# Cross-attention with layer norm: score products of 32 rows instead of 64

## The chip, the core and the metric

The kernel runs on one NeuronCore of a Trainium2 chip. The metric is the time of one execution on the device in microseconds. Five engines work side by side, each through its own list of instructions in order: PE (TensorE, with its weight loads shown apart as PEld), DVE (VectorE), ACT (ScalarE), POOL (GpSimd) and SP (SyncE, which here only issues transfers).

## The reference, cut to what matters

```python
qs  = (q @ wq).reshape(B, S, 16, 32).transpose(0, 2, 1, 3)      # q: 4 x 2048 x 512
ks_ = (k @ wk).reshape(B, 77, 16, 32).transpose(0, 2, 1, 3)     # k = v: 4 x 77 x 512
vs  = (v @ wv).reshape(B, 77, 16, 32).transpose(0, 2, 1, 3)
scores = einsum('bhqd,bhkd->bhqk', qs, ks_) / sqrt(32)
scores = where(mask[:, None, :, :], -inf, scores)
attn_w = softmax(scores, axis=-1)
attn = einsum('bhqk,bhkd->bhqd', attn_w, vs)
out  = attn.transpose(0, 2, 1, 3).reshape(B, S, 512) @ wo + q
return layernorm(out) * gamma + beta
```

There are 8,192 query rows, 16 heads of 32 channels, and 77 keys for each of the four batches. The scores are, for each head and query row, a sum over only 32 channels.

## The kernel before

The 8,192 rows are worked on as 64 tiles of 128 rows. Keys and values are made once at the start. Queries are projected for four tiles at a time (`q_rows`, L276), transposed: a head's 32 channels lie on 32 partitions, four heads above each other, so that `q_g` holds heads in four groups of rows (`j` = 0 to 3) and four groups along its free dimension (`g` = 0 to 3). The weights and activations of the large products are split into a high and a low part and multiplied in three terms.

For one tile these steps follow each other, on several engines:

- `scores` (L406, PE): 16 heads by 77 keys. The queries are the loaded operand, the keys `kct` the moving one, 77 columns. The products read 32 partitions, so they take 32 of the array's rows; the rows of the tile are taken `SR` at a time, and each product writes `SR` partitions of one of four banks of PSUM (`sc[j]`, one bank for each group of partitions). With `SR` = 64 there are 32 products for a tile, in eight places of the array (4 groups of rows x 2 groups of 64 columns).
- `maxima` (L423, DVE): adds the mask, negates and copies the scores of one head to SBUF and gives their minimum; 16 instructions for a tile. The banks come free with it.
- `exps` (L438, ACT): 16 exponentials with row sums.
- `recip` and `normalise` (L448 DVE, L453 POOL), then `transp` (L474, DVE) transposes in blocks of 32, and twelve transfers for two tiles (`regroup_part`, L485) put the keys on partitions.
- `av` (L499, PE): weights by values for two tiles, 96 rows by 32 columns of the array for each product, four places side by side; then ACT and DVE split the result (L528, L532).
- `o_proj` (L555, PE): 12 products of 128 x 512 for a tile, then residual, layer norm and store on DVE, POOL, ACT and SP.

The order of all this on all engines is written out by hand in one list of words (`ORDER`): `S5` are the scores of tile 5, `T5.0` to `T5.3` its maxima, `V2` the value products of tiles 4 and 5, `O7` the output projection of tile 7, `Q14` a part of a query projection. A second table (`SLOTS`) names the buffer or the PSUM bank that each tile gets. In most places PE's list has one `S` between other products; four times two stand in a row (S0 S1, S2 S3, S6 S7, S56 S57). An instruction that needs a bank waits in PE's list until DVE or ACT has read it.

The products of one tile are issued by this loop; `SR` is the constant that the change touches, and nothing else in the program uses it:

```python
        for g in range(NG):
            for r0 in range(0, P, SR):
                for j in range(GH):
                    q = slice(HD * j, HD * (j + 1))
                    mm = nc.tensor.matmul(
                        sc[j][r0 : r0 + SR, g * NK : (g + 1) * NK],
                        qs[q, g, rs.start + r0 : rs.start + r0 + SR],
                        kct[q, g, t // TPB, keys_of(j)],
                        start=True,
                        stop=True,
                    )
```

The innermost loop goes over the four groups of partitions `j`, the next over the rows of the tile, the outermost over the four groups of heads.

Of the kernel before, what the change touches and what calls it, by code (L numbers as in the profile page):

```python
# [38 lines left out]
MASKED = -3.38e38  # L39
EPS = 1.0e-5  # L40
WARM = 9
SR = 64
NPB = 3
KSCALE = 1.0 / HD**0.5
LAST = 56
# [129 lines left out]
def xattn_layernorm(  # L175
# [75 lines left out]
    def keys_of(h):  # L251
        return slice(TAIL_K, NK2) if h % 2 == 0 else slice(0, NK)
# [145 lines left out]
    def scores(t):  # L398
# [3 lines left out]
# [8 lines that stand above are left out]
# [388 lines left out]
```

## Time and profile before

| | before |
|---|---|
| median of 2 runs | 511.21 us (510.82 to 511.6) |
| profiled execution | 511.52 us |
| its span, first to last instruction | 509.7 us |
| mean granted TensorE clock | 0.996 |
| PE busy | 499.7 us, 6,833 matmuls, as many loads |
| DVE, ACT, POOL busy | 468.1, 465.1, 420.9 us |
| HBM traffic | 41.79 MB read, 16.78 MB written |

How to read the profile: a line of a group names the source line, the engine, the operation, and written tile <- read tiles; for PE the form `32*64` is how many rows and columns of the array the product takes, `32x77` what moves through it. Behind it stand the count, the busy time and the mean of one, and the idle time of the engine ahead of these instructions with what ended it. A row of waits names who waited for what, the total in us, how often, and the longest. PE's matmuls overlap: the next one starts while the one before is still running out, so the sum of their durations is more than the time they take. A tile's score products stand in the trace as a burst, a row of loads and matmuls of line 406 without anything between.

### The profile page before, as it was taken

How to read it: one execution, taken by the hardware profiler on the slowest of the kernel's cores; microseconds unless marked ns; L12 is line 12 of the kernel's file. 1: busy time of each engine (PE TensorE's matmuls, PEld its weight loads, DVE VectorE, ACT ScalarE, POOL GpSimd, SP SyncE). 2: the span in 40 equal slices, each digit the busy share in tenths (PEclk: the TensorE clock that was granted, in tenths of full speed). 3: DMA queues.
4: the chain of work that ended last, by engine and by line, in shares of the span. 5: the costliest groups of instructions: out<-in, count | busy, mean ns of one | idle time of the engine just before them, and what ended most of it. 6: DMA issues, size and time to landing. Idle time of an engine off the chain costs nothing. (4 is left out here: it accounts for less than half of the span.)

```text
span 509.7 us, 20305 instructions
## 1 busy us (share of the span) xinstructions
PE 499.7 (98%) x6833; PEld 383.9 (75%) x6833; DVE 468.1 (92%) x2559; ACT 465.1 (91%) x2222; POOL 420.9 (83%) x387
## 2 busy tenths in 40 slices
PE   8999999999999999999999999999999999999994
PEld 6987878777777778777777777777777777777773
DVE  6799989998998989889989998999999999999997
ACT  6699999999999999998999999999999999989620
POOL 3656566866897999997998898998999899998895
PEclk9999999999999999999999999999999999999998
DMA  8947877778688975879787878787978688689655
GB/s 297 395 169 204 184 202 185 187 184 241 185 232 232 253 214 144 231 214 270 215 251 200 219 187 236 192 223 194 249 215 209 194 225 236 194 220 255 160 187 215
DMA packets 58781, 110.85 MB, mean 217 GB/s; under 512 B 9462, under 2 KB 11278, under 8 KB 58678
## 3 DMA queue, kind: packets, MB, share of 16 engines
q1 hardware_dynamic: 55222, 102.75, 72.4%
q0 software_dynamic: 2496, 5.77, 4.2%
q10 hardware_dynamic: 960, 1.05, 0.8%
q8 instruction: 54, 0.88, 0.8%
q14 instruction: 49, 0.40, 0.3%
HBM read 41.79 MB, written 16.78 MB: 115 GB/s over the span
## 5 line engine op out<-in xcount | busy, mean ns | idle before, releaser
L438 ACT ACTIVATE pbuf<-pbuf,nm 128x77 f32<-128x77 f32 x1024 | 352.7, 352 | 8.0 <-DVE nm L423 7.7
L438 ACT ACTIVATION_READ_ACCUMULATOR pbuf<-pbuf,nm 128x1 f32 x1024 | 197.3, 193 | 0.0
L423 DVE CUSTOM_DVE_ANT_0 pbuf<-sc,mb 128x77 f32<-128x77 f32 x1024 | 170.2, 233 | 6.9 <-PE sc L406 4.8
L453 POOL TENSOR_TENSOR pbuf<-pbuf,ri 128x1232 f32<-128x1232 f32 x63 | 142.4, 2264 | 34.1 <-DVE ri L448 28.6
L474 DVE STREAM_TRANSPOSE B<-pbuf 128x1280 f32<-128x1280 f32 x64 | 95.9, 1500 | 9.2 <-POOL pbuf L453 7.0
L555 PE MATMUL po<-woh,AH 128*128 128x512 f32 x256 | 104.0, 406 | 0.1
L276 PE MATMUL pq<-xth,wqh 128*128 128x512 f32 (+1 forms) x256 | 100.6, 393 | 0.8 <-DVE nm L423 0.7
L555 PE MATMUL po<-wol,AH 128*128 128x512 f32 x256 | 100.0, 391 | 0.0
L555 PE MATMUL po<-woh,AL 128*128 128x512 f32 x256 | 99.9, 390 | 0.0
L276 PE MATMUL pq<-xtl,wqh 128*128 128x512 f32 (+1 forms) x256 | 98.2, 383 | 0.0
L276 PE MATMUL pq<-xth,wql 128*128 128x512 f32 (+1 forms) x256 | 98.1, 383 | 0.0
L423 DVE DVE_READ_ACCUMULATOR2_ANT nm<- 128x1 f32 x1024 | 85.9, 84 | 0.0
L270 POOL TENSOR_TENSOR xtl<-xtf,xth 128x1024 fp32r<-128x1024 f32 x28 | 67.4, 2406 | 10.5 <-ACT xth L266 7.2
L596 POOL TENSOR_TENSOR o<-o,gam 128x512 f32<-128x512 f32 x56 | 72.2, 1294 | 2.6 <-ACT o L593 2.6
L599 POOL TENSOR_TENSOR o<-o,bet 128x512 f32<-128x512 f32 x56 | 72.0, 1291 | 1.4
L406 PEld LDWEIGHTS sc<-kct,q 32*64 32x64 f32 x4096 | 51.7, 130 | 22.2 <-issue 12.0
L406 PE MATMUL sc<-kct,q 32*64 32x77 f32 x4096 | 61.3, 238 | 0.3 <-DVE nm L423 0.2
L499 PE MATMUL pa<-PT,vsb 96*32 96x256 f32 x992 | 59.7, 382 | 0.2 <-DMA PT<-B 0.2
L555 PEld LDWEIGHTS po<-woh,AH 128*128 128x128 f32 x256 | 48.0, 188 | 15.2 <-issue 3.2
L276 PEld LDWEIGHTS pq<-xth,wqh 128*128 128x128 f32 x256 | 48.1, 188 | 14.7 <-issue 2.5
L555 PEld LDWEIGHTS po<-woh,AL 128*128 128x128 f32 x256 | 48.1, 188 | 10.6
L276 PEld LDWEIGHTS pq<-xth,wql 128*128 128x128 f32 x256 | 48.1, 188 | 9.8
(99 smaller groups left out, 638.2 us busy)
## 6 DMA issues: line engine op xcount, KB each, us to landing
PT<-B SPq DMA_DIRECT2D x343, 128.0 KB
xtf<-xT SPq DMA_DIRECT2D x28, 512.0 KB
o<-x SPq DMA_DIRECT2D x56, 256.0 KB
out<-o SPq DMA_DIRECT2D x56, 256.0 KB
PT<-B POOLq DMA_DIRECT2D x25, 128.0 KB, 4.8
stage_a<-kin SPq DMA_DIRECT2D x4, 410.0 KB
xtf<-xT SPq DMA_DIRECT2D x4, 256.0 KB
wq_f<-wq SPq DMA_DIRECT2D x4, 256.0 KB
```

The lines of the kernel that those rows point to most:

```text
L270: return nc.gpsimd.tensor_tensor(l[:, c : c + 2], fx.pop((g, c)), xh[g][:, c : c + 2].bitcast(F32), ALU.subtract)
L276: nc.tensor.matmul(pq, w[:, c, m * P : (m + 1) * P], r[g][:, c, rs], start=(n == 0), stop=(n == 11))
L406: mm = nc.tensor.matmul(sc[j][r0 : r0 + SR, g * NK : (g + 1) * NK], qs[q, g, rs.start + r0 : rs.start + r0 + SR], kct[q, g, t // TPB, keys ...
L423: nc.vector.tensor_tensor_reduce(pb[:, h // 2, (h % 2) * NK : (h % 2 + 1) * NK], scs[t][j][:, g * NK : (g + 1) * NK], mb[:, t % TPB, keys_ ...
L438: nc.scalar.activation(pb[:, h // 2, (h % 2) * NK : (h % 2 + 1) * NK], pb[:, h // 2, (h % 2) * NK : (h % 2 + 1) * NK], AF.Exp, bias=nmax[t ...
L453: return nc.gpsimd.tensor_tensor(pv, pv, rv.to_broadcast((P, NP, 2, NK)), ALU.mult)
L474: nc.vector.transpose(bt.rearrange("p c q r -> p q c r"), pbuf[t % NPB].rearrange("p q (c r) -> p q c r", c=5),)
L499: nc.tensor.matmul(pas[b, g // 2][HD * j : HD * (j + 1), (g % 2) * BLK : (g % 2 + 1) * BLK], vsb[:, 2 * b // TPB, h % 2, HD * (h // 2) : H ...
L555: nc.tensor.matmul(pos[t], a[:, c, rs], w[:, c, :], start=(first and c == 0 and n == 0), stop=(c == NC_D - 1 and n == 2),)
L596: return nc.gpsimd.tensor_tensor(od[t], od[t], gam, ALU.mult)
L599: return nc.gpsimd.tensor_tensor(od[t], od[t], bet, ALU.add)
```

## The change

One constant: the rows of a tile that one score product takes.

```diff
 EPS = 1.0e-5
 WARM = 9
-SR = 64
+SR = 32
 NPB = 3
```

The loop over `r0` now takes four steps instead of two. Each product loads 32 columns of queries instead of 64 and writes 32 partitions instead of 64; the keys that move through are the same 77 columns. A tile has 64 products instead of 32, and they lie in sixteen places of the array (4 groups of rows x 4 groups of 32 columns) instead of eight. All products of one group `j` still write one bank, and the sixteen products of one `g` follow each other before the next `g`. The words of the order, the banks and buffers, and the lists of the other engines are what they were; on PE's list 5,850 program matmuls stand where 3,802 stood, and each of the new ones stands beside the one that it was cut from or four places on.

## The prediction

> **What bounds the kernel now.** I read the busy table first, then the same busy times by stage, then who waits for whom, and last the inside of one burst of score products.
>
> ```profile
> PE 499.7 (98%) x6833; PEld 383.9 (75%) x6833; DVE 468.1 (92%) x2559; ACT 465.1 (91%) x2222; POOL 420.9 (83%) x387
> ...
> 0.00:20.00 20.00, 18.57 (x123) 15.83 (x124) 12.84 (x27) 12.84 (x26) 7.11 (x19) 1.00 0.95 336
> 20.00:465.00 445.00, 443.81 (x6381) 340.17 (x6381) 415.69 (x2435) 432.89 (x2124) 377.46 (x316) 1.00 0.79 214
> 465.00:509.70 44.70, 37.37 (x343) 27.95 (x340) 39.58 (x100) 19.34 (x75) 36.32 (x53) 0.96 0.67 195
> ```
>
> The columns of the windows are the stretch, its length, then PE, weight loads, DVE, ACT and POOL (busy time and number of instructions), the granted clock, and the DMA. From 20 to 465 us, where all scores lie (20.9 to 465.6, in line 406's row below), TensorE is busy 443.8 of 445.0 us. ACT has 432.9 us of work there and DVE 415.7, so they are close behind, but behind.
>
> A busy PE could still be a waiting PE, so the waits come next:
>
> ```profile
> PEld sc L406 <- issue: 12.0, 34, 0.4
> PEld sc L406 <- DVE nm L423: 6.0, 15, 0.5
> DVE pbuf L423 <- PE sc L406: 4.8, 11, 1.0
> ```
>
> The idle time of weight loads ahead of scores is about 0.35 to 0.4 us each time, whoever is named: this is the pause in which the array empties before the first 32-row load, and it comes once per burst. No single wait is longer than 0.5 us. TensorE works through its order and waits for nobody; whatever makes its part of one tile longer is added to the end, 64 times.
>
> Now the line that changes, its loads, and the one other place with 32-column loads:
>
> ```profile
> L406 PEld LDWEIGHTS sc<-kct,q 32*64 32x64 f32 x4096 | 51.7, 130 | 22.2 <-issue 12.0 <-DVE nm L423 6.0 <-DVE ri L448 0.8
> L406 PE MATMUL sc<-kct,q x4096: 222/225/277, 20.9 to 465.6; 32*64 32x77 f32 x196
> L499 PEld LDWEIGHTS pa<-PT,vsb x992: 106/110/110, 68.4 to 485.2; 96*32 96x32 f32 x199
> L499 PE MATMUL pa<-PT,vsb x992: 376/379/403, 68.4 to 485.4; 96*32 96x256 f32 x199
> ```
>
> The program has 64 tiles x 32 = 2,048 score products, the trace 4,096 pairs of a load and a matmul: each f32 product runs as two pairs, a first pass and a second pass in the same place of the array. One burst is 64 pairs:
>
> ```profile
> 205.06 0.80 PEld L406 LDWEIGHTS sc<-kct,q 32*64 32x64 f32 x64 [0.35 <-PE pq L276]
> 205.06 0.95 PE L406 MATMUL sc<-kct,q 32*64 32x77 f32 x64
> ```
>
> That is 0.95 us from first start to last end; a matmul takes 0.225, so the last starts 0.726 us after the first. How these starts lie is read from windows that all begin at 205.00, before the burst, so that the counts (matmuls, then loads) add up:
>
> ```profile
> 205.00:205.11 0.11, 0.05 (x8) 0.05 (x8) 1.00 0.86 261
> 205.00:205.16 0.16, 0.10 (x8) 0.10 (x16) 1.00 0.58 176
> 205.00:205.19 0.19, 0.13 (x10) 0.13 (x18) 1.00 0.55 172
> 205.00:205.38 0.38, 0.32 (x33) 0.32 (x33) 1.00 0.83 226
> 205.00:205.43 0.43, 0.37 (x33) 0.37 (x34) 1.00 0.78 219
> 205.00:205.44 0.44, 0.38 (x33) 0.38 (x35) 1.00 0.76 214
> 205.00:205.48 0.48, 0.42 (x37) 0.42 (x37) 1.00 0.75 213
> 205.00:205.68 0.68, 0.62 (x54) 0.62 (x61) 1.00 0.80 223
> 205.00:205.80 0.80, 0.74 (x64) 0.74 (x64) 1.00 0.80 225
> ```
>
> Three rates are in here. **Start rate**: 16 loads from 205.06 to 205.16, 15 gaps of 6.7 ns. **Place rate**: from 205.19 to 205.38 23 matmuls start in 0.19 us, 8.3 ns each, that is one round of all eight places per 0.067 us. Then the third: by 205.38 33 loads have begun, the 34th just after, and then nothing until the 35th at 205.44. From 205.48 to 205.68 the loads come at 24 in 0.20 us, 8.3 ns each, so one product (two loads) per 16.7 ns; this is a **supply rate**, since the first of these go to places that stand idle and still come one product at a time.
>
> Why does the 35th load wait? Four times two tiles' bursts stand behind one another; one such pair shows whether the pause repeats:
>
> ```profile
> 420.50:420.52 0.02, 0.00 (x0) 0.00 (x0) 1.00 0.62 205
> 420.50:420.55 0.05, 0.01 (x3) 0.02 (x3) 1.00 0.52 164
> 420.50:420.90 0.40, 0.36 (x33) 0.37 (x34) 1.00 0.12 31
> 420.50:420.92 0.42, 0.39 (x35) 0.39 (x35) 1.00 0.11 29
> 420.50:421.28 0.78, 0.74 (x67) 0.75 (x68) 1.00 0.06 16
> 420.50:421.30 0.80, 0.77 (x69) 0.77 (x69) 1.00 0.06 15
> ...
> 421.77 0.52 PE L406 MATMUL sc<-kct,q 32*64 32x77 f32 x25
> ...
> 420.50:422.10 1.60, 1.56 (x128) 1.57 (x128) 1.00 0.29 111
> ```
>
> Load 1 starts at 420.54, load 35 at 420.91 (between 420.90 and 420.92), load 69 at 421.29. So load n+34 comes 0.375 us after load n, twice in a row, and the same 0.375 separates 205.06 from 205.44. I read it as a **window**: 34 pairs, or 17 products, are all that may be under way, and a product leaves it when its second pass has ended. The parts fit: second pass begins 0.117 us after the product's first load (the ninth matmul, between 205.16 and 205.19), lasts 0.225, and some 0.03 is left for the next to arrive: 0.375.
>
> **The change, part by part.** Each of the 32 products of a tile becomes two of 32 rows: 64 products, 128 pairs, per tile; 8,192 pairs in all in place of 4,096. The moving operand stays at 77 columns, the loads shrink from 64 to 32 columns, the places go from eight to sixteen. No other engine gets or loses an instruction, no transfer and no bank changes, and the order is the same.
>
> What shrinks: the first load before the first pass. It shows as 277 against 225 ns at L406, 52 ns with 64 columns, and as 403 against 379 at L499, 24 ns with 32. So a second pass starts 0.117 - 0.027 = 0.090 us after its product's first load, and the window's turn is 0.375 - 0.027 = 0.348 us. Later loads run under matmuls and cost nothing; without that cover it would be 0.02 to 0.05 us for each pass, and the place rate above shows the cover is there (0.067 us a round, with a 0.131 us load per matmul).
>
> What the sixteen places give: the place rate no longer binds, since 17 products hardly more than fill the array once. What then binds is the window. Counting products from 0: product 17 begins at 0.348 us, product 34 at 0.696, product 51 at 1.044, each after the window's turn; inside each batch the products come 16.7 ns apart (17 x 16.7 = 0.284, shorter than the turn, so the turn decides). Product 63 is the twelfth after 51: 1.044 + 12 x 0.0167 = 1.244. Its second pass: + 0.090 = 1.334 us.
>
> The same bookkeeping on the burst of before, to test it: product 17 at 0.375, product 31 fourteen later, + 0.234, + 0.117 for its second pass: 0.726. Measured: 0.726.
>
> So a burst grows from 0.726 to 1.334 us, by 0.608. The pause ahead (0.35) and the emptying behind it stay. All 64 count, since TensorE is the bound in the whole stretch: 64 x 0.608 = 38.9 us. In the four pairs that stand back to back the batches run on (128 products: product 119 at 7 x 0.348 = 2.436, eight more at 16.7 ns, + 0.090 = 2.66, against 1.53 now, 421.77 + 0.52 - 0.225 - 420.54), which is 1.13 in place of 1.22 more: -0.3 us for all four. Sum: 38.6 us.
>
> The work of DVE on a tile (L423) waits for the tile's scores and will begin 0.6 us later each time; that shows as idle time of DVE, and costs nothing while PE is the bound: DVE's 415.7 and ACT's 432.9 us stand in a stretch that grows to some 484. Nothing stands behind it but the softmax of that tile, whose results PE needs several bursts later.
>
> Bounds. From below: if only the start rate held, 127 x 6.7 ns = 0.851, + 0.125, 64 times + 8.0 us. From above: the nearest row to 128 pairs is the back-to-back pair of tiles, 1.53 us on eight places with a wait for banks in it: + 0.80, 64 times + 51 us. I take the window's value between them, since it repeats twice and gives 0.726 for the burst of before.
>
> The profiled execution took 511.52 us (span 509.7, the rest around it), 0.3 above the median of 511.21; I work from its own time: 511.5 + 38.6 = **550 us**.
>
> A rule speaks against this. The Trainium skill, TensorE: Matmul & The Clock Gate, Part 3: Packing small matmuls, gives a pack's span as one matmul plus about 4 ns for each further tile, and its measured gain is largest with all sixteen tiles. By it 128 pairs would need an estimated 0.225 + 127 x 0.004 = 0.73 us, less than the 0.95 that 64 pairs take now. The trace does not bear it out here: no gap below 6.7 ns in the burst, and 8.3 after it.
>
> **The rivals.**
>
> *The array decides after all; faster.* Mechanism: 128 pairs on sixteen places are eight rounds, as 64 on eight are. Without the window a burst is 0.090 + six more rounds of 0.067 + sixteen starts of a last round at 4.2 ns (0.067/16) = 0.56 us, 0.17 less than now: 64 x 0.17 = 10.9, **500.6 us**. It decides from a mean start gap below 0.726/127 = 5.7 ns. For it: the place rate of 0.067 does bind in the first half of a burst now. Against it: 6.7 ns is the shortest gap, even at L499's 32-column loads, and the 35th load waits with places idle. Faster than some 499 it cannot be, since ACT's 432.9 us leave 12 of the 445. That rule of the skill would land here.
>
> *Only the start rate; no change.* If small products leave the window as fast as they start: + 8.0 us, **519.5**. Against it: the supply rate.
>
> *The supply rate alone.* One pause, then 16.7 ns a product without a second one: 0.348 + 46 x 0.0167 + 0.090 = 1.206 us, + 0.48, 64 times 30.7: **542**. For it: a single burst of before shows only one pause. Against it: load 69 at 421.29; but a wait for a bank stands near it and could be what I see.
>
> *The worse side.* Loads that do not get shorter leave the turn at 0.375: product 51 at 1.125, 63 at 1.325, end 1.442: + 0.716, 45.8 us, **557**. And fetching code:
>
> ```profile
> q8 instruction: 54, 0.88, 0.8%
> ```
>
> 0.88 MB for 13,666 loads and matmuls is 64 B each, so 8,192 more are 0.52 MB, 32 more fetches of 16 KB. A fetch lasts 0.008 x 16 x 509.7/54 = 1.2 us; if every new one were waited for, + 39 us on top, **589**. Against it: 54 are hidden now.
>
> **How the numbers follow.** Window: 0.62, 550 (its own range 546 to 554). Supply alone: 0.18, 542. Start rate alone: 0.06, 519.5. Array decides: 0.03, 500.6. The worse side: 0.11, mostly 557. The range 536 to 559 takes in the window, the supply case with a shorter first pause, and the longer loads, and leaves out the two cheap cases, the fetches and the upper bound. A measurement of this kernel can tell about 2% (10 us) from no change: faster 0.03, same 0.06, slower 0.91, from the same cases.
>
> **What would show it.** Right: line 406 with 8,192 pairs of form 32*32, loads of 106 to 110 ns in place of 130, bursts of about 1.56 us in place of 0.95; in cumulative counts, pauses before loads 35, 69 and 103, 0.35 us apart; PE still busy over 97% from 20 to some 500 us; DVE waiting for scores longer than 4.8 us in all. Supply alone: one pause, bursts of 1.43. Start rate alone: 1.08 and no pause. Wrong altogether: bursts below 0.95 us, or bursts as I say and a PE that had idle time to give, which the waits of weight loads would then show gone.

## The result, and the profile after

| | before | after |
|---|---|---|
| median of 2 runs | 511.21 us | 601.64 us (598.02 to 605.27) |
| ratio | | 1.1767 [1.173, 1.1805] |
| profiled execution, its span | 511.52, 509.7 us | 598.02, 596.2 us |
| mean granted clock | 0.996 | 0.980 |
| PE busy | 499.7 us (98%) | 555.5 us (93%) |

Runs that lie more than 1.5% above the fastest of the same kernel count as slow, and times are compared without them.

The change makes the kernel 18% slower, 90 us. The prediction said slower, but by 38.6 us and to at most 559: it missed by 52 us. The page of the profile after, its busy table, its line of code fetches, and the groups of the score products:

```profile
PE 555.5 (93%) x10929; PEld 427.7 (72%) x10929; DVE 470.8 (79%) x2559; ACT 468.7 (79%) x2222; POOL 421.1 (71%) x387
...
q8 instruction: 86, 1.41, 1.1%
...
L406 PE MATMUL sc<-kct,q 32*32 32x77 f32 x8192 | 106.5, 237 | 25.0 <-issue 25.0
L406 PEld LDWEIGHTS sc<-kct,q 32*32 32x32 f32 x8192 | 89.0, 103 | 52.9 <-issue 41.6
```

8,192 pairs of form 32*32 are there, with loads of 103 ns and 86 code fetches in place of 54, the 32 more that the prediction counted. New is the end of the row of matmuls: 25.0 us of idle time ahead of these matmuls, all under "issue", the name for time in which the engine waited for nothing that the profile shows. The table of waits (engine, line, what it waited for; us in all, how often, the longest) says how this idle time is shaped:

```profile
DVE pbuf L423 <- PE sc L406: 56.7, 42, 4.2
...
PEld sc L406 <- issue: 41.6, 54, 4.7
PE sc L406 <- issue: 25.0, 15, 4.6
PEld pa L499 <- issue: 12.7, 13, 3.0
PE pa L499 <- issue: 6.8, 7, 2.6
```

Before, loads waited for "issue" 12.0 us, 34 times, at most 0.4 us. Now single waits last up to 4.7 us, they stand at the value products (L499) too, and DVE, which waited 4.8 us for scores, waits 56.7. The engine that waited for nobody now stands still by itself.

**The inside of a burst is as predicted.** The timeline of one undisturbed burst after (start, length, group), and cumulative windows that all begin at 244.00, restricted to line 406 (columns as in the prediction's windows, PE and weight loads only):

```profile
244.09 1.38 PEld L406 LDWEIGHTS sc<-kct,q 32*32 32x32 f32 x128 [0.35 <-PE pq L276]
244.09 1.56 PE L406 MATMUL sc<-kct,q 32*32 32x77 f32 x128
```

```profile
244.00:244.37 0.37, 0.28 (x33) 0.23 (x34) 1.00 1.05 327
244.00:244.44 0.44, 0.35 (x35) 0.30 (x35) 1.00 1.04 335
244.00:244.77 0.77, 0.68 (x66) 0.63 (x68) 1.00 0.98 340
244.00:244.79 0.79, 0.70 (x68) 0.65 (x69) 1.00 0.97 337
244.00:245.13 1.13, 1.04 (x101) 0.99 (x102) 1.00 0.97 343
244.00:245.15 1.15, 1.06 (x103) 1.01 (x104) 1.00 0.97 346
```

The pauses stand before loads 35, 69 and 103, 34 apart, at about 244.43, 244.78 and 245.14: one turn of 0.35 us after the other. First to last start is 1.337 us, the forecast was 1.334.

**The rest are holes.** The timeline of 37.3 to 40.9 us, in which a tile's products are cut in two (PE, then the loads behind the hole; the counts are those of this window), and the transfers in 38.0 to 40.6 us:

```profile
37.06 1.21 PE L406 MATMUL sc<-kct,q 32*32 32x77 f32 x90
40.52 0.62 PE L406 MATMUL sc<-kct,q 32*32 32x77 f32 x37 [2.25 <-issue]
40.52 0.47 PEld L406 LDWEIGHTS sc<-kct,q 32*32 32x32 f32 x37 [2.44 <-issue]
```

```profile
DMA packets 1, 0.02 MB, mean 6 GB/s; under 512 B 0, under 2 KB 0, under 8 KB 0
q8 instruction: 1, 0.02, 2.3%
```

PE stops in the middle of a tile's products for 2.5 us. In that time this core moves a single packet: 16 KB of code, on queue q8, at 38.19 to 39.15; PE goes on at 40.52, 1.4 us behind its end.

Where in the program do these holes lie? Windows from 0 to the beginning of a hole count the matmuls and loads done until then:

```profile
0.00:22.96 22.96, 21.77 (x350) 19.15 (x351) 14.47 (x37) 13.46 (x29) 10.21 (x21) 1.00 0.97 344
0.00:38.06 38.06, 32.31 (x605) 28.48 (x606) 21.45 (x101) 25.91 (x92) 14.05 (x22) 0.91 0.80 284
0.00:72.27 72.27, 64.28 (x1241) 53.70 (x1241) 48.56 (x257) 50.80 (x225) 32.55 (x30) 0.95 0.69 216
```

701, 1,211 and 2,482 instructions: 510 apart, then 1,271. With the few waits that PE's list holds besides (they are not in the counts) these are 2 x 256 and 5 x 256. A fetch of 16 KB at 64 B is 256 instructions. Counted through all that the trace records of PE, loads, matmuls and waits, every long hole ends at an instruction that is 193 past a multiple of 256: at the border of two blocks of code. A hole is counted here where at such a border a matmul starts more than 0.25 us behind the one before it and the block's packet has just landed. There are 27 of them, of 0.27 to 4.8 us, 40.2 us together; in the kernel before there is none. In every one the block's packet ends 1.2 to 1.7 us before PE goes on; at the borders of the kernel before, it ended at least 2.5 us ahead.

How long a block takes differs. Windows from a border to the start of the next block's packet, for the three longest holes and for the one at 38.06:

```profile
21.57:25.47 3.90, 1.59 (x153) 1.42 (x138) 1.99 (x24) 2.98 (x17) 2.97 (x2) 1.00 1.15 381
36.67:38.18 1.51, 1.51 (x151) 1.42 (x139) 0.71 (x6) 1.51 (x5) 0.00 (x0) 1.00 0.00 0
188.78:191.40 2.62, 2.48 (x127) 1.66 (x128) 1.46 (x17) 2.62 (x16) 2.61 (x2) 1.00 0.85 230
398.93:404.17 5.24, 4.91 (x127) 3.48 (x126) 4.80 (x24) 4.59 (x25) 4.87 (x4) 1.00 0.92 274
```

The last column but one is the DMA's busy share. With the DMA idle in this stretch (eight of the holes) the packet starts at most 1.5 us behind the border and PE goes on at most 3.9 us behind it. Each of the seven starts that come later than that, up to 5.3 us, falls where the DMA is busy (share 0.84 or more). The lateness goes with other transfers, then; that they hold the packet up was not tested.

**Behind some long holes the clock falls.** Windows on a hole of 3.2 us that begins at 191.03, on the time behind it, and on two of 2.5 us, which begin at 72.25 and 497.89:

```profile
191.00:194.20 3.20, 0.26 (x20) 0.07 (x9) 1.51 (x1) 3.20 (x13) 3.20 (x4) 0.83 0.66 211
194.80:199.20 4.40, 4.40 (x11) 3.43 (x12) 4.11 (x29) 4.04 (x24) 2.88 (x3) 0.50 0.67 153
70.25:73.66 3.41, 2.23 (x168) 1.99 (x166) 2.47 (x10) 1.90 (x11) 0.00 (x0) 1.00 0.72 162
73.66:77.07 3.41, 2.23 (x62) 1.85 (x63) 1.43 (x18) 1.06 (x7) 0.00 (x0) 1.00 0.56 150
496.91:500.33 3.42, 1.21 (x110) 1.04 (x100) 2.82 (x26) 2.37 (x15) 1.24 (x2) 1.00 0.88 265
500.33:503.74 3.41, 3.32 (x72) 2.69 (x72) 2.67 (x25) 3.41 (x21) 3.39 (x4) 0.50 0.94 277
```

The third column from the end is the granted clock: 0.50 for the 4.4 us of the second row, in which only 11 large products run, 427 ns from start to start where it is 227 elsewhere. One hole of 2.5 us brings it to 0.50, the other leaves it at 1.00.

The last four rows show why. In this trace the clock changes only at steps of 3.41 us (it falls at 25.87, 408.17 and 500.33, which are 112 and 27 such steps apart). The hole at 72.25 lies across two steps and leaves PE idle for 1.2 us in each; the one at 497.89 lies almost wholly in one and leaves it idle for 2.2 us there. From 20 us on, the clock fell behind every step at full clock with some 1.9 us or more without a matmul, and behind none with 1.5 us or less; in the four experiments below that are in float32 and have holes, the two bounds are 1.8 and 1.5.

Behind the holes at 191.0, 403.6 and 497.9 there are 27 slowed products, some 0.2 us more each, 5.4 us; behind the longest, of 4.8 us at 22.9, 19 products of half the size start 213 instead of 118 ns apart, 1.8 us.

The sum: 64 bursts x 0.611 (1.337 - 0.726) = 39.1, holes 40.2, half clock 7.2: 86.5 us. The span grew by 596.2 - 509.7 = 86.5. The parts are not sure to the tenth (some 0.2 us of a hole is the usual distance between large products), and that the sum meets to the tenth is luck; but nothing of size is missing.

### The profile page after: what moved, and what is told of

Read it like the earlier page. It is cut to its first block, busy times and chain, and to the rows that moved or that the text cites. A ratio compares the mean times of both kernels' runs of the same rounds, so it can differ in the third digit from the quotient of the medians.

```text
span 596.2 us, 28496 instructions
## 1 busy us (share of the span) xinstructions
PE 555.5 (93%) x10929; PEld 427.7 (72%) x10929; DVE 470.8 (79%) x2559; ACT 468.7 (79%) x2222; POOL 421.1 (71%) x387
## 5 line engine op out<-in xcount | busy, mean ns | idle before, releaser
L423 DVE CUSTOM_DVE_ANT_0 pbuf<-sc,mb 128x77 f32<-128x77 f32 x1024 | 170.7, 232 | 57.3 <-PE sc L406 56.7
L438 ACT ACTIVATION_READ_ACCUMULATOR pbuf<-pbuf,nm 128x1 f32 x1024 | 194.9, 190 | 0.0
L406 PE MATMUL sc<-kct,q 32*32 32x77 f32 x8192 | 106.5, 237 | 25.0 <-issue 25.0
L406 PEld LDWEIGHTS sc<-kct,q 32*32 32x32 f32 x8192 | 89.0, 103 | 52.9 <-issue 41.6
L276 PE MATMUL pq<-xth,wqh 128*128 128x512 f32 (+1 forms) x256 | 102.6, 401 | 0.0
L276 PE MATMUL pq<-xtl,wqh 128*128 128x512 f32 (+1 forms) x256 | 99.9, 390 | 0.0
L276 PE MATMUL pq<-xth,wql 128*128 128x512 f32 (+1 forms) x256 | 99.7, 390 | 0.0
L499 PE MATMUL pa<-PT,vsb 96*32 96x256 f32 x992 | 64.2, 383 | 6.9 <-issue 6.8
L528 ACT CAST AH<-pa 128x512 fp32r<-128x512 f32 x64 | 36.5, 577 | 34.8 <-PE pa L499 27.6
L276 PEld LDWEIGHTS pq<-xth,wqh 128*128 128x128 f32 x256 | 49.5, 194 | 14.4 <-issue 2.7
L276 PEld LDWEIGHTS pq<-xth,wql 128*128 128x128 f32 x256 | 49.6, 194 | 10.0
```

The lines of the kernel that those rows point to most:

```text
L276: nc.tensor.matmul(pq, w[:, c, m * P : (m + 1) * P], r[g][:, c, rs], start=(n == 0), stop=(n == 11))
L406: mm = nc.tensor.matmul(sc[j][r0 : r0 + SR, g * NK : (g + 1) * NK], qs[q, g, rs.start + r0 : rs.start + r0 + SR], kct[q, g, t // TPB, keys ...
L423: nc.vector.tensor_tensor_reduce(pb[:, h // 2, (h % 2) * NK : (h % 2 + 1) * NK], scs[t][j][:, g * NK : (g + 1) * NK], mb[:, t % TPB, keys_ ...
L438: nc.scalar.activation(pb[:, h // 2, (h % 2) * NK : (h % 2 + 1) * NK], pb[:, h // 2, (h % 2) * NK : (h % 2 + 1) * NK], AF.Exp, bias=nmax[t ...
L499: nc.tensor.matmul(pas[b, g // 2][HD * j : HD * (j + 1), (g % 2) * BLK : (g % 2 + 1) * BLK], vsb[:, 2 * b // TPB, h % 2, HD * (h // 2) : H ...
L528: nc.scalar.copy(*at_part(once(ahs, b, [P, NG, BLK], F32R, "AH"), b, i, by_tile))
```

## The experiments

The theory after the result: **late code**. PE's list is fetched in blocks of 256 instructions, hardly further ahead than one block, and a block is ready some 5 us after it is asked for. One burst of 64 products is 256 loads and matmuls, a whole block, and is used up in 1.35 us. Rivals: the holes come with the form of the product (sixteen places, 32 columns, waits at banks); each burst pays for its length wherever it lies; or it is the amount of code, each fetch at a price. Working this theory through PE's list (each burst, value product and large product at its measured rate; a block is asked for when PE takes in the one ahead, which I set 64 instructions before their start, and is ready a fixed time later) gives 28 holes with 39.8 us for the kernel after at 5.0 us, and none for the kernel before. So the 5 us are fitted; what it says of other kernels is not. It leaves out that a block is later where the DMA is busy. All kernels ran beside the kernel before (511.0 to 511.4 us).

### Every product of 64 rows twice

```diff
-SR = 32
+SR = 64
...
-            for r0 in range(0, P, SR):
+            for r0 in [r for r in range(0, P, SR) for _ in range(2)]:
```

The tile again has 64 products, but on eight places and with loads of 64 columns, each row step issued twice in a row.

> The kernel before (64 rows, eight places) with each score product issued twice over: as many products, passes and instructions on PE as in the changed kernel, but none in the 32*32 form. Theory A (two costs that come from the number of products in a burst: the window of 34 pairs, and code that is fetched in blocks of 256 PE instructions and is late when a burst eats a block in 1.4 us): pauses before loads 35, 69 and 103 of a burst with a turn of 0.375 us, undisturbed bursts of 1.44 us from first to last start, and holes of 0.4 to 5 us every 256 PE instructions, some 40 us in all, as after. Sum 511.5 + 64 x 0.716 + 40 = 597 us (588 to 606). Rival B (the holes come with the sixteen places or the 32-column loads): no holes, 557 us. Rival C (the holes are waits for banks that DVE frees late because the bursts end late): holes as in A, but not at a fixed step of instructions.

Measured: 604.26 us (a second run took 614.67); 86 fetches; 20 holes, 30.8 us. That is as slow as the change, without anything of sixteen places. The burst was off: the first to the last start takes 1.58 us, not 1.44.

```profile
246.37 1.80 PE L406 MATMUL sc<-kct,q 32*64 32x77 f32 x128
```

The repeated product stands four products behind the first on the same place, so that the 17 products under way lie on only four or eight places; the order of the products, which I had taken not to matter, would then count. The next kernel tests this.

### All products of 64 rows, then all again

```diff
-SR = 32
+SR = 64
...
-            for r0 in range(0, P, SR):
+            for r0 in [*range(0, P, SR)] * 2:
```

> Each 64-row product issued twice, as in the first run, but the second time only after all eight places have had their turn (there the two stood next to each other, so that the pairs in the window covered four places and a burst took 1.58 us in place of the 1.44 expected). Window of 34 pairs: pauses before loads 35, 69 and 103, 0.375 us apart, bursts of 1.44 us, only the turn (0.375 against 0.348) longer than in the changed kernel; with late code (27 holes, 37 us worked out for a latency of 5 us) and a lower clock behind the longest holes, 600 us (590 to 612). Rival (what held up the first run was its 64 columns, not its order): 1.58 us again. Rival (a limit of the places, 16 rounds of 0.067): 1.1 to 1.2 us.

Measured: 603.31 us (602.21 to 604.42), ratio 1.1808 [1.1747, 1.1868]; 26 holes, 37.2 us. Windows on one burst (line 406 only, from 247.60):

```profile
247.60:248.09 0.49, 0.36 (x33) 0.37 (x34) 1.00 0.92 351
247.60:248.11 0.51, 0.39 (x35) 0.39 (x35) 1.00 0.89 337
247.60:248.46 0.86, 0.73 (x66) 0.74 (x68) 1.00 0.95 360
247.60:248.48 0.88, 0.76 (x68) 0.76 (x69) 1.00 0.94 358
247.60:248.83 1.23, 1.10 (x100) 1.11 (x102) 1.00 0.98 366
247.60:248.86 1.26, 1.14 (x102) 1.14 (x103) 1.00 0.99 369
```

Loads 35, 69 and 103 again, now 0.375 us apart, the turn of the kernel before; the last start comes 1.444 us after the first, as forecast: it was the order. The form of before with the number of products of after gives the time of after (601.6). Neither sixteen places nor 32-column loads cost anything that these runs can show; they even save 0.027 us a turn. The loss is the number of instructions, through the window and through the code.

### 128 rows: half as many products as before

```diff
-SR = 32
+SR = 128
```

> 128 rows for a product: 16 products, 32 pairs in a burst, four places, loads of 128 columns. Theory A: all pairs fit in the window and PE gets 4,096 instructions fewer, so neither pause nor hole; the place decides, by its load (128 columns, 0.027 us for each 32 by the change from 130 to 103 ns: 0.107) and not by its stream of 0.064: 0.107 + 0.064 + six rounds of 0.109 + 0.02 = 0.85 us in place of 0.726, + 8 us, 519 (514 to 524). Rival (fewer instructions is all that counts): eight rounds of 0.067, 0.56 us, - 10 us, 501. Rival (the load does not run under the stream of its place: 0.171 a round): 1.3 us, + 37 us, 548.

Measured: 520.24 us (519.43 to 521.16), ratio 1.0172 [1.0147, 1.0197]; 38 fetches, no hole.

```profile
209.18 0.98 PEld L406 LDWEIGHTS sc<-kct,q 32*128 32x128 f32 x32 [0.35 <-DVE B L474]
209.18 1.13 PE L406 MATMUL sc<-kct,q 32*128 32x77 f32 x32
```

32 pairs fit into the window of 34, and no pause shows; there the four places bind, with a round of 0.111 us and loads of 186 ns, and the burst's starts span 0.861 us, 0.135 more than before: 64 x 0.135 = 8.6 us, measured 9. So, in float32, 64 rows lie between two bounds, places on one side and pairs on the other.

### 32 rows, keys and queries in bfloat16; and 64 rows likewise

```diff
-    kct = const.tile([P, NG, NB, NK2], F32, name="kct")
+    kct = const.tile([P, NG, NB, NK2], BF16, name="kct")
...
-            nc.vector.tensor_copy(once(qd, g, [P, NG, GRP], F32, "q")[:, m, :], pq)
+            nc.vector.tensor_copy(once(qd, g, [P, NG, GRP], BF16, "q")[:, m, :], pq)
```

and the same for the first `q`. A product is then one pair in place of two; the scores lose the precision of float32. With `SR` = 32 a burst is 64 pairs, as before, on sixteen places:

> 32 rows, sixteen places, but keys and queries of the scores are rounded to bf16, so that each product runs as one pass (64 pairs in a burst, as many as before; the scores lose precision). Theory A: no late code, since a burst is 128 instructions again and the program is no longer than before; the window counts pairs, so the pause comes before load 35, at 0.024 (load) + 0.032 (half of the 0.064 stream) + 0.161 + 0.03 = 0.25 us, then 8.3 ns a pair: burst 0.50 us in place of 0.726. 64 x 0.226 = 14.5 less, but ACT has 433 us of work in 445, so some 500 us (496 to 505). If the window counts products, the pause comes before load 18 and the burst is 0.7 us: 510. Rival B (sixteen places are slow or holey by themselves): above 520.

Measured: 507.3 us (506.73 to 508.83), ratio 0.9922 [0.9899, 0.9945].

```profile
203.32 0.69 PE L406 MATMUL sc<-kct,q 32*32 32x77 bf16 x64
```

```profile
203.20:203.54 0.34, 0.22 (x32) 0.21 (x33) 1.00 0.75 229
203.20:203.57 0.37, 0.25 (x35) 0.23 (x35) 1.00 0.74 221
```

The burst takes 0.490 us to its last start, with the pause at load 34 after 0.238 us. The same places and the same 64 products as in the change, with half the instructions: one hole, of 2.8 us, where the expectation had none. The time missed the forecast's upper end by 2 us; that hole and the work of ACT are the likely causes, not tested apart. With `SR` = 64:

> The kernel before with keys and queries of the scores rounded to bf16: one pass for a product, 32 pairs in a burst on eight places (the scores lose precision). Theory A: all in the window, four rounds of 0.053 to 0.067: bursts of some 0.25 us; PE would save 64 x 0.47 = 30 us, but ACT (433 us of work in 445) and DVE then bound: 495 to 502. Against the run with 32 rows it shows what 32 more pairs cost where code and passes are few: nothing on the time, 0.25 us in the burst.

Measured: 505.44 us (504.72 to 506.38), ratio 0.9882 [0.9862, 0.9902].

```profile
PE 471.6 (94%) x4785; PEld 351.6 (70%) x4785; DVE 463.9 (92%) x2559; ACT 463.5 (92%) x2222; POOL 420.7 (84%) x387
```

The burst fell to 0.150 us and the time by 6 us, not by 64 x 0.576 = 37: PE, busy 94%, now waits for DVE and ACT. My forecast had this bound 3 us too low. It also says what a burst is worth at most: from 0.490 us to 0.150 the time fell by 2 us only.

### 32 rows in half the tiles, chosen by the theory

Two kernels with the same number of products, of fetches (70 in each) and of tiles with 32 rows; only which tiles these are differs. In the first they are chosen so that the theory finds almost no late block, in the second so that it finds many:

```diff
-SR = 32
+SR = 64
+SR32 = {0, 3, 4, 8, 9, 10, 11, 14, 16, 19, 20, 22, 24, 26, 29, 30, 31, 33, 35, 37, 38, 41, 42, 43, 44, 45, 48, 49, 50, 54, 55, 61}
...
+        sr = 32 if t in SR32 else SR
...
-            for r0 in range(0, P, SR):
+            for r0 in range(0, P, sr):
```

> 32 rows for 32 of the 64 tiles, 64 rows for the others; the tiles are chosen so that no burst of 128 pairs falls on a boundary of a block of 256 PE instructions whose successor was asked for less than 5 us before. Theory A (a block is asked for when the one ahead of it is entered, and is there 5 us later; the latency is the one that gives 28 holes and 39.8 us when it is worked out for the changed kernel, 27 and 40.2 measured): 1 hole of 1 to 2 us; 32 x 0.611 = 19.6 for the window; sum 533 us (529 to 538). Rival (each burst of 128 pairs costs its share of the holes wherever it stands): 511.5 + 86.5/2 = 555. Rival (the window is not what makes the undisturbed burst 0.611 longer, or PE had time to give): below 525.

Measured: 543.21 us (542.85 to 544.39), ratio 1.0623 [1.0598, 1.0648]. The other choice, `{0, 1, 3, 5, 6, 7, 8, 12, 13, 14, 18, 21, 22, 24, 28, 29, 34, 36, 37, 38, 43, 44, 45, 47, 48, 51, 52, 56, 57, 58, 59, 60}`:

> As many tiles with 32 rows as in the quiet choice (32 of 64), as many PE instructions and the same undisturbed bursts, but chosen so that as many boundaries of blocks as can be fall into or right behind a burst of 128 pairs. Theory A: 21 holes, 37 us (26 to 48 for a latency of 4.5 to 5.5 us), with the window's 19.6: 569 us (557 to 581), 36 more than the quiet choice. Rival (cost by burst): 555 like the other. Rival (waits for banks, or the amount of code): no difference between the two.

Measured: 565.99 us; three other runs took 574.48, 575.89 and 579.85, at a granted clock of 0.973, 0.971 and 0.969 against 0.991. The trace is of the run of 574.48. In both kernels line 406 has become 408. Loads that waited for "issue", first choice:

```profile
PEld sc L408 <- issue: 17.7, 40, 2.7
```

and second choice:

```profile
PEld sc L408 <- issue: 39.2, 51, 4.6
```

Holes at block borders: 10 with 11.2 us against 19 with 33.7 us. The two kernels do the same work with the same number of instructions, and 23 us lie between 543.21 and 565.99. This is what neither the amount of code nor a price of each burst can give: what counts is how soon after one border the next comes. The second lies in its forecast of 557 to 581; how many holes that fastest run had is not on record. The first is 10 us slower than the 533, and its 11.2 us of holes are why: 511 + 32 x 0.611 + 11.2 = 542. The theory had expected one hole and got ten. Its timing is too coarse to place borders that come near the limit: in the first kernel 3.2 to 6.6 us passed from one border to the end of the hole at the next, not 5.0 each time.

## Why the prediction was wrong, point by point

**The bound.** Right: PE set the end, and what lengthens its part is added to it. But PE's busy share fell to 93%, where more than 97% was expected: from 20.6 to 552.6 us it is busy 499 of 532. The line that no single wait is longer than 0.5 us holds for the scores' loads; one load at L276 waited 0.8 us, which changes nothing.

```profile
20.60:552.60 532.00, 499.44 (x10519) 383.77 (x10518) 419.94 (x2438) 439.67 (x2141) 379.88 (x319) 0.98 0.68 182
```

**The window.** Right, in count and size: pauses before loads 35, 69 and 103, a turn of 0.348 us with loads of 32 columns and of 0.375 with 64, bursts of 1.337 us for 1.334, so 39.1 us for 38.9. The rivals that let the array, the start rate or the supply alone decide are out by the same windows.

**The rule on packs.** The Trainium skill, TensorE: Matmul & The Clock Gate, Part 3: Packing small matmuls, gives about 4 ns for each further tile. In float32 that does not hold here: the mean from first to last start is 1.337/127 = 10.5 ns, and the first twelve matmuls start 6.7 ns apart. In the bfloat16 kernel of 32 rows the first twelve do start 3.3 ns apart.

**The step that failed** is the sentence on the worse side: "if every new one were waited for, + 39 us on top, 589. Against it: 54 are hidden now". The holes measure 40.2 us, and 589 is 13 us from the result. The argument against it was not one. That 54 fetches are hidden says nothing of how narrowly. The profile before had the answer: its shortest block, 256 instructions from border to border in 4.55 us (the row counts also those that reach in from outside),

```profile
353.81:358.36 4.55, 4.32 (x129) 2.72 (x135) 4.33 (x25) 4.46 (x19) 4.24 (x8) 1.00 0.79 203
```

against the 1.56 us of a whole burst of 256 instructions that the prediction itself foresaw. A block would be used up three times as fast as ever before, and the prediction did not ask how long a fetch has from request to use; it took the 1.2 us of the packet alone. The packets after last 0.9 to 1.7 us too, and yet blocks come late: up to 5.3 us from the border ahead to the packet's start, and the 1.2 to 1.7 us behind its end, come on top.

Not each new fetch is waited for: 27 of 86 borders hold a hole. At all of them PE had used up the block between in 1.35 to 5.2 us, and at least 189 of its 256 instructions were score products; at ten other borders that came as soon, the code was there in time or nearly so. That the sum of 40.2 us lies near the price of 32 fetches at 1.2 us is chance.

The Trainium skill, Runtime: NRT & Kernel Launch, section Instruction fetch mechanics, says that the sequencer fetches the next page of 256 instructions while the present one runs, so that the cost is mostly hidden. The blocks of 256 agree with the trace; "mostly hidden" held for the kernel before and not after, with 27 holes of 0.27 to 4.8 us.

**The clock** stood in no step. The Trainium skill, TensorE: Matmul & The Clock Gate, Part 1, has the clock halved after an idle window of some 3.4 us. Here the granted clock was 0.50 behind holes of 4.8, 3.2 and 2.5 us, so a shorter stop was enough.

**The range** of 536 to 559 took in the window's uncertainties only, and gave the fetches, the longer loads and all else on that side together 0.11. A cost with a known price and no measured margin should have widened it upward to the 589.

**What stays open:** what frees a place in the window, of which only the count and the turn are shown; and why one block is there 2.2 us behind the border ahead of it and another only 7.9, of which the part that goes with a busy DMA is seen, but not shown to come from it.

## What to carry to other kernels

Before cutting a product into smaller ones, count the instructions in the burst and put them against two numbers of the trace: how many pairs may be under way, and how many instructions one block of code holds. A cost that is hidden now is worth a look at its margin: take the shortest time in which PE uses up a block, before and after, from one border to the next. Any 256 instructions will not do: before, the four pairs of bursts that stand in a row used up as many in some 1.7 us without a hole, since a border fell inside each (at 22.0, 29.2, 58.2 and 421.2 us). Where an engine's waits are named "issue" and lie at a constant step in its instruction count, it is likely to be waiting for code, whatever its line in the source does.

## What the runs showed of the hardware

- PE's code comes in blocks of 256 instructions. At the 27 late ones of the kernel after, PE went on 2.2 to 3.9 us behind the border before where the DMA was idle up to the packet's start, and up to 7.9 us behind it where it was busy. PE restarts 1.2 to 1.7 us after the packet's end.
- A long hole in PE, of 2.5 us for one, can cost twice: the granted clock is then 0.50 for one or two steps of 3.41 us, and large products start every 427 ns instead of 227. What counted was the idle time within one step: in the float32 kernels 1.8 us and more brought the clock down, 1.5 and less did not. One of the lines of L276 in 194.2 to 200 us:

```profile
L276 PE MATMUL pq<-xtl,wqh 128*128 128x512 f32 x4 | 2.5, 628 | 0.0
```

  628 ns for one, against 389 at full clock (the median of this line's matmuls in both kernels).
- At most 34 pairs of a load and a matmul are under way on PE, with 32 columns as with 64, in float32 (two pairs a product); in bfloat16 the pause came before load 34.
